# Two bilinear corner sums per sample instead of three, for a part of a deformable convolution's samples

## The chip, the cores and the metric

The kernel runs on one core of a Trainium2 chip (trn2). The metric is the device time of one execution in microseconds. The engines are written PE (TensorE), DVE (VectorE), ACT (ScalarE), POOL (GpSimd) and SP (SyncE); PEld is PE's weight load.

## The reference, cut to what matters

Four layers run one after the other on x of shape (2, 256, 64, 64) in float32, numbered 0 to 3: attention, a position term, a bottleneck with a deformable convolution, and the layer of this case, two deformable convolutions in a row:

```python
def bilinear_gather(x, py, px):
    y0, x0 = jnp.floor(py), jnp.floor(px)
    wy1, wx1 = py - y0, px - x0
    wy0, wx0 = 1.0 - wy1, 1.0 - wx1
    ...
    return (gather(y0, x0) * (wy0 * wx0)[:, None] + gather(y0, x0 + 1.0) * (wy0 * wx1)[:, None]
        + gather(y0 + 1.0, x0) * (wy1 * wx0)[:, None] + gather(y0 + 1.0, x0 + 1.0) * (wy1 * wx1)[:, None])

def deform_conv(x, dw, pw, pwb, w, b):
    f = lax.conv_general_dilated(x, dw, (1, 1), 'SAME', feature_group_count=C, dimension_numbers=dn)
    off = lax.conv_general_dilated(f, pw, (1, 1), 'SAME', dimension_numbers=dn)
    ...
    sampled = bilinear_gather(x, py, px)
    return jnp.einsum('bckhw,ock->bohw', sampled, w.reshape(O, C, KK)) + b[None, :, None, None]

h = deform_conv(jax.nn.relu(group_norm(x, gn1_g, gn1_b)), dw1, pw1, pwb1, w1, b1)
h = deform_conv(jax.nn.relu(group_norm(h, gn2_g, gn2_b)), dw2, pw2, pwb2, w2, b2)
return h + x
```

Each of 9 taps of each pixel is read at a fractional place: four neighbours, each with the product of a weight in y and a weight in x. The weights differ from pixel to pixel and are the same for all 256 channels.

## The kernel before, in words

The third layer is the method `deform`. It keeps the normalised image in memory as rows that hold, for a place, the 256 channels of two lines of the image, so that one indexed read of 4 KB per pixel brings all four corners: `four`, 128 pixels by 4 x 256 channels, in the order (left, upper), (left, lower), (right, upper), (right, lower). Such a tile is the unit of the work and is called a sample here: one tap for 128 pixels. `parts(s)` takes the number s of a sample apart: n is the convolution and image (four of them, `layers`: first convolution of image 0, of image 1, then the second of each), i one of 8 blocks of 512 pixels, k the tap and j the quarter of a block. There are 36 samples in a block, 288 in a convolution of an image, 1152 in all.

The order of work on PE, ACT, DVE and POOL is written out by hand: it is the order in which the program issues instructions, and each engine runs its own in that order. The loop at L1570 has one step for each s:

- `gather(s + 8)`: an indexed read on POOL's queue (line 846) into one of ten buffers `four`. The first two blocks of image 0 were sampled during layer 0 and come by plain transfers from `samp_d` on SP's queue instead.
- `first(s + 1)`: ACT multiplies corner 0 by its weight into a new tile `smp` (L1459); there are five such tiles.
- `others(s)`: DVE multiplies and adds corners 1, 2 and 3 one after the other (L1465).
- every fourth step `evacuate`: ACT copies four transposed samples from PSUM (L1486).
- `product`: PE multiplies with the convolution's weights (L1496, two instructions in the records for each call), then `turn(s - 2)`: PE transposes a sample (L1477, two instructions). A `turn` frees its `smp`.
- what is due: at the end of a block an activation (L1521) or a residual add on DVE (L1532).
- side work in small portions: the offsets of later blocks (`offsets`: PE at L803, L823 and L837, ACT at L814 and L832), from which `corners` computes indices and weights on DVE (L738 to L776); the next image (`image`: ACT L1370, PE L1380, DVE L1386); and at the start of the layer what remains of layer 2's deformable convolution for image 1 (`seconds`: POOL L846, DVE L1065 to L1076).

`corners` first has the weights by axis, `w` with one entry per side (0 is left or upper, 1 is right or lower) and axis (0 is y, 1 is x), and then the four products `w4`, of which `first` and `others` use one per corner. The tile `w` lies in a work pool and is overwritten by the next block but one; `w4` and the indices lie in a pool of four, `cp`.

Of the kernel before, what the change touches and what calls it, by code (L numbers as in the profile page):

```python
# [11 lines left out]
F32 = mybir.dt.float32  # L12
# [3 lines left out]
ALU = mybir.AluOpType  # L16
# [4 lines left out]
P = 128  # L21
B, C, H, W = 2, 256, 64, 64
# [3 lines left out]
K2 = 9  # L26
# [3 lines left out]
EARLY = 2  # L30
# [34 lines left out]
class Net:  # L65
# [662 lines left out]
                n += 2  # L728


    def corners(self, i, pt, mask, base, idx, w4, pool):

        nc = self.nc
        p = pool.tile([P, 4, K2, 2], F32, name="pos")
        off = pt[:, :, 0 : 2 * K2].rearrange("p j (k t) -> p j k t", t=2)
        nc.vector.tensor_tensor(p, off, base[:, 4 * i : 4 * i + 4], ALU.add)  # L738
        if mask:
            mk = pool.tile([P, 4, K2], F32, name="mask")  # L740
            nc.vector.tensor_scalar_max(mk, pt[:, :, 2 * K2 : 3 * K2], -87.0)
        yield False
        if mask:

            nc.scalar.activation(mk, mk, AF.Exp, scale=-1.0)

        nc.vector.tensor_scalar(p, p, float(H), -1.0, ALU.min, ALU.max)
        whole = pool.tile([P, 4, K2, 2], I32, name="whole")
        nc.vector.tensor_copy(whole, p)
        yield True  # L750
        f = pool.tile([P, 4, K2, 2], F32, name="floor")
        nc.vector.tensor_copy(f, whole)
        g = pool.tile([P, 4, K2, 2], F32, name="above")
        nc.vector.tensor_tensor(g, f, p, ALU.is_gt)
        yield False
        nc.vector.tensor_tensor(f, f, g, ALU.subtract)
        nc.vector.tensor_scalar_min(f, f, float(H - 1))
        w = pool.tile([P, 2, 4, K2, 2], F32, name="wt")
        nc.vector.tensor_tensor(w[:, 1], p, f, ALU.subtract)
        yield False  # L760
        nc.vector.tensor_scalar(w[:, 0], w[:, 1], -1.0, 1.0, ALU.mult, ALU.add)
        at = pool.tile([P, 4, K2], F32, name="at")
        nc.vector.scalar_tensor_tensor(
            at, f[:, :, :, 0], float(GW), f[:, :, :, 1], ALU.mult, ALU.add
        )
        nc.vector.tensor_scalar_add(idx, at, float(GW + 1))
        yield True
        if mask:
            nc.vector.tensor_scalar_add(mk, mk, 1.0)
            nc.vector.reciprocal(mk, mk)  # L770
            yield False
            for s in range(2):
                nc.vector.tensor_mul(w[:, s, :, :, 1], w[:, s, :, :, 1], mk)
            yield False
        for s in range(4):
            nc.vector.tensor_mul(w4[:, :, :, s], w[:, s % 2, :, :, 0], w[:, s // 2, :, :, 1])  # L776
        yield True
# [8 lines left out]
            ALU.mult,  # L786
        )

    def offsets(self, i, srcs, wt, bias, base, idx, w4, pool, wide, ps, odp=None, y0=0, later=lambda f: f()):

        nc, half, size = self.nc, DWK // 2, DWK
        m = size * 2 * K2
        pd = ps([P, 512])
        order = [half] + [t for t in range(size) if t != half]
        n = 0
        for s, src in enumerate(srcs):
            for t in order:  # L800
                y = 8 * i + t - half
                r0, r1 = max(0, -y), min(8, H - y)
                nc.tensor.matmul(  # L803
                    pd[:m, r0 * W : r1 * W],
                    lhsT=wt(s, t),
                    rhs=src[:, (y + r0 - y0) * W : (y + r1 - y0) * W],
                    start=(n == 0),
                    stop=(n == len(srcs) * size - 1),
                )
                n += 1  # L810
                yield "bank"

        later(
            lambda: nc.scalar.copy(  # L814
                wide[:m, :, half : half + W], pd[:m].rearrange("p (r w) -> p r w", w=W)
            )
        )
        yield
        pz = ps([P, 512])
        sums = pz.rearrange("p (r w) -> p r w", w=W)  # L820
        for t in range(size):
            g = t % 4
            nc.tensor.matmul(  # L823
                sums[32 * g : 32 * g + 32],
                lhsT=self.shift[:m, t, :],
                rhs=wide[:m, :, t : t + W],
                start=(t < 4),
                stop=(t + 4 >= size),
            )
        yield "bank"  # L830
        od = odp() if odp else pool.tile([P, 512], F32, name="od")
        later(lambda: nc.scalar.activation(od, pz, AF.Identity, bias=bias))  # L832
        yield

        pt = ps([P, 4, 32])
        for j in range(4):
            nc.tensor.matmul(  # L837
                pt[:, j, :], lhsT=od[:, j * P : (j + 1) * P], rhs=self.sel, start=True, stop=True
            )
        yield "bank"  # L840
        for _ in self.corners(i, pt, False, base, idx, w4, pool):
            yield

    def gather(self, dst, img, idx):
# [9 lines left out]
    class Bottleneck:  # L854
# [41 lines left out]
            self.od = wp.tile([P, 512], F32, name="bod")  # L896
            nc.gpsimd.memset(self.od, 0.0)

        def pools(self, ctx, gathers=5):
            self.ahead = gathers - 1  # L900
            tc = self.net.tc
            return self.kept | {
                n: ctx.enter_context(tc.tile_pool(name=f"bt_{n}", bufs=bufs))
                for n, bufs in (("g", gathers), ("s", 8), ("t", 6), ("x", 2))
            }

        def block(self, pool, src, i):
# [391 lines left out]
    def deform(self, bott):  # L1299
# [4 lines left out]
        tc, nc, a = self.tc, self.nc, self.a  # L1304
        with ExitStack() as ctx:
            gp = ctx.enter_context(tc.tile_pool(name="df_g", bufs=10))
            wp = ctx.enter_context(tc.tile_pool(name="df_w", bufs=1))
            work = ctx.enter_context(tc.tile_pool(name="df_work", bufs=2))
# [87 lines left out]
                        yield  # L1396

            IMAGE = 4 + 6 * NB + 1
            corners = {(0, 0, i): (None, w4) for i, w4 in self.early.items()}

            def offsets(b, l):
                if b == 0:
                    yield from offset_weights(l)
                wf = self.wf
                for i in range(EARLY if (b, l) == (0, 0) else 0, NB):
                    idx = cp.tile([P, 4, K2], I32, name="didx")
                    w4 = cp.tile([P, 4, K2, 4], F32, name="dw4")
                    corners[b, l, i] = idx, w4
                    yield from self.offsets(
                        i,  # L1410
                        [x[b][:, cb, :] for cb in range(2)],
                        lambda s, row: wf[:, s, DWK * row : DWK * row + DWK, :].rearrange(
                            "p t o -> p (t o)"
                        ),
                        self.vec[:, V_PWB + l : V_PWB + l + 1],
                        base, idx, w4, work, ods[i % 2], pd,
                    )

            ods = [wp.tile([P, 8, W + DWK - 1], F32, name=f"wide{n}") for n in range(2)]
# [10 lines left out]
            def parts(s):  # L1430
                n, r = divmod(s, LAYER)
                i, r = divmod(r, BLOCK)
                return n, i, r // 4, r % 4

            def gather(s):
                if s < ALL:
                    n, i, k, j = parts(s)
                    b, l = layers[n]
                    fours[s] = gp.tile([P, 4, C], F32, name="four")
                    four = fours[s].rearrange("p s c -> p (s c)")  # L1440
                    if n == 0 and i < EARLY:

                        queue = nc.gpsimd if s < AHEAD else nc.sync
                        m = 4 * k + j
                        queue.dma_start(four, self.samp_d[i][m * P : m * P + P, :])
                        return
                    idx = corners[b, l, i][0]
                    self.gather(four, self.img3[b], idx[:, j, k : k + 1])

            def weight(s, c):  # L1450
                n, i, k, j = parts(s)
                w4 = corners[(*layers[n], i)][1]
                return w4[:, j, k, c : c + 1]

            def first(s):

                if s < ALL:
                    smps[s] = sp.tile([P, C], F32, name="smp")
                    nc.scalar.mul(smps[s], fours[s][:, 0], weight(s, 0))  # L1459

            def others(s):
                if s < ALL:
                    four = fours.pop(s)
                    for c in range(1, 4):
                        nc.vector.scalar_tensor_tensor(  # L1465
                            smps[s], four[:, c], weight(s, c), smps[s], ALU.mult, ALU.add
                        )
# [83 lines left out]

            OFFS = 24
            inner = ExitStack()
            second = bott.conv(1, bott.pools(inner, 8), ps)
            for s in range(AHEAD):
                gather(s)
                conv_weight(0, s)
# [12 lines left out]
            for s in range(ALL + 12):  # L1570
                n = s // LAYER
                if s == LAYER:
                    stats[1] = self.norm_stats()
                gather(s + AHEAD)
                first(s + 1)
                others(s)
                if (s - 6) % 4 == 0:
# [126 lines left out]
```

## Time and profile before

| | us |
|---|---|
| median of 3 runs | 5151.03 (5145.72 to 5154.88) |
| profiled execution, first to last instruction (its span) | 5149.0 |
| DVE busy in it | 4196.7 (82%) |
| PE busy | 4816.8 (94%) |
| ACT busy | 2883.6 (56%) |
| POOL busy | 2254.7 (44%) |
| L1465, the three corner additions: 3240 + 216 instructions of 128x256 | 1503.8 + 104.4 |
| L1459, the first corner: 1080 + 72 of 128x256 | 535.9 + 34.3 |
| third layer's first sample, from the trace (L1459) | 2995.4 |

The busy time of an engine is the time in which at least one of its instructions runs; instructions of one engine can overlap at their ends. For PE the ends are modelled, so its busy share is not its share of peak. The profiled execution has no time of its own beside its span; the median of the runs stands 2 us above it. A windowed view gives busy time in a stretch, with the count of instructions in brackets.

### The profile page before, as it was taken

The page shows a single profiled execution, that of the slowest core. Times are in us where ns is not written, and L with a number is a line of the kernel's source. Part 1 is how long each engine was busy: PE and PEld are TensorE (multiplying, and loading weights), DVE is VectorE, ACT ScalarE, POOL GpSimd, SP SyncE. Part 2 cuts the span into 40 slices and gives each one's busy share as a digit, 9 for nine tenths or more (in the row PEclk, how much of TensorE's full clock was granted, in tenths as well). Part 3 has the DMA queues.
Part 4 walks back from the last instruction along what each step waited for, and adds up shares of the span by engine and source line. Part 5 has one row for each costly group of instructions (what it writes and reads, how often), then busy time and mean ns, then how long its engine had stood idle before and what let it go on. Part 6 is the DMA issues. An engine that isn't in the chain of part 4 may idle for free. (4 is left out here: it accounts for less than half of the span.)

```text
span 5149.0 us, 100000 instructions
## 1 busy us (share of the span) xinstructions
PE 4816.8 (94%) x38200; PEld 2651.9 (52%) x38200; DVE 4196.7 (82%) x7929; ACT 2883.6 (56%) x5221; POOL 2254.7 (44%) x2256
## 2 busy tenths in 40 slices
PE   8999999999999999999999957679999999999998
PEld 5555565555565555565555523234444444444443
DVE  6878867878668888687766768878999999999998
ACT  5666656666666666666656622235444554454444
POOL 0111111111107777464023257775666566666665
PEclk9999999999999999999999967789999999999999
DMA  5231121111113333322557677679999999999998
GB/s 172 61 99 51 42 68 49 35 46 30 55 52 94 93 100 102 94 85 79 150 193 272 233 242 239 207 251 376 340 329 339 360 359 350 356 388 346 347 348 318
DMA packets 367022, 997.66 MB, mean 194 GB/s; under 512 B 61372, under 2 KB 98810, under 8 KB 366542
## 3 DMA queue, kind: packets, MB, share of 16 engines
q0 software_dynamic: 196560, 690.41, 37.7%
q1 hardware_dynamic: 169438, 300.73, 17.9%
q8 instruction: 300, 4.92, 0.4%
q14 instruction: 180, 1.47, 0.1%
q10 hardware_dynamic: 544, 0.13, 0.0%
HBM read 855.36 MB, written 127.35 MB: 191 GB/s over the span
## 5 line engine op out<-in xcount | busy, mean ns | idle before, releaser
L1465 DVE SCALAR_TENSOR_TENSOR smp<-four,dw,smp 128x256 f32<-128x256 f32 x3240 | 1503.8, 483 | 122.3 <-ACT smp L1459 44.4
L598 ACT ACTIVATE e<-sc,low 128x1024 f32<-128x1024 f32 x1024 | 1147.1, 1120 | 745.1 <-DVE low L592 741.4
L592 DVE TENSOR_REDUCE low<-sc 128x1 f32<-128x1024 f32 x1024 | 1204.8, 1218 | 228.1 <-PE sc L580 224.0
L846 POOL DMA_INDIRECT four<-img,didx x1080 | 1085.4, 1005 | 646.3 <-DVE smp L1465 349.2
L1496 PE MATMUL out<-st,wc 128*128 128x512 f32 x2304 | 1229.6, 616 | 65.0 <-ACT st L1486 33.6
L580 PE MATMUL sc<-k,qs 64*128 64x512 f32 x2048 | 997.1, 605 | 1.8 <-ACT e L598 1.4
L639 PE MATMUL av<-et,v 128*64 128x256 f32 x8192 | 996.5, 385 | 0.0
L580 PE MATMUL sc<-k,q 64*128 64x512 f32 x2048 | 977.3, 604 | 0.0
L519 POOL TENSOR_TENSOR o<-o,f 128x1024 f32<-128x1024 f32 x63 | 149.3, 2370 | 1771.5 <-DMA f<-share_d 890.1
L610 PEld LDWEIGHTS tt<-ident,e 64*128 64x128 f32 x16384 | 651.7, 139 | 519.3 <-issue 275.4
L1459 ACT ACTIVATE smp<-four,dw 128x256 f32<-128x256 f32 x1080 | 535.9, 507 | 594.3 <-PE pt L1477 460.4
L610 PE MATMUL tt<-ident,e 64*128 64x64 f32 x16384 | 726.1, 226 | 40.5 <-ACT et L629 19.9
L629 ACT COPY et<-tt 128x512 f32<-128x512 f32 x1152 | 659.5, 586 | 170.5 <-PE tt L610 169.2
L627 DVE COPY et<-tt 128x512 f32<-128x512 f32 x896 | 612.0, 683 | 161.3 <-PE tt L610 160.9
L639 PEld LDWEIGHTS av<-et,v 128*64 128x64 f32 x8192 | 552.1, 137 | 302.9 <-issue 48.4
L1477 PEld LDWEIGHTS pt<-ident,smp 128*128 128x128 f32 x2304 | 320.5, 144 | 740.8 <-issue 423.4
L846 POOL DMA_INDIRECT bfour<-img,bidx x576 | 581.0, 1009 | 184.2 <-issue 90.3
L1496 PEld LDWEIGHTS out<-st,wc 128*128 128x128 f32 x2304 | 392.0, 196 | 323.3 <-issue 216.5
L1477 PE MATMUL pt<-ident,smp 128*128 128x128 f32 x2304 | 454.6, 280 | 72.7 <-DVE smp L1465 67.1
L580 PEld LDWEIGHTS sc<-k,qs 64*128 64x128 f32 x2048 | 345.4, 188 | 215.7 <-issue 120.0
L1486 ACT COPY st<-pt 128x1024 f32<-128x1024 f32 x288 | 291.2, 1011 | 289.5 <-PE pt L1477 287.8
L803 PE MATMUL pd<-x,wf 128*126 128x512 f32 x840 | 433.4, 598 | 0.0
(183 smaller groups left out, 3600.4 us busy)
## 6 DMA issues: line engine op xcount, KB each, us to landing
f<-share_d SPq DMA_DIRECT2D x128, 256.0 KB
four<-samp_d SPq DMA_DIRECT2D x64, 512.0 KB
xb<-xn SPq DMA_DIRECT2D x55, 512.0 KB
img<-imgt SPq DMA_DIRECT2D x96, 256.0 KB
four<-img,didx POOLq DMA_INDIRECT x1080, 6.1
xa<-res SPq DMA_DIRECT2D x32, 512.0 KB
samp_d<-xb SPq DMA_DIRECT2D x32, 512.0 KB
xb<-in_x SPq DMA_DIRECT2D x20, 512.0 KB
```

The costliest lines, as they stand in the source:

```text
L580: nc.tensor.matmul(s[:, j, :], lhsT=q[u, i // 2][int(h != j)][halves[j], at : at + P], rhs=k[u][c][halves[j], h, :], start=True, stop=True,)
L592: nc.vector.tensor_reduce(low, s, AX.X, ALU.max, negate=True)
L598: nc.scalar.activation(e.rearrange("p j n -> p (j n)"), s, AF.Exp, bias=blk.low[:, g, c : c + 1], accum_out=blk.sum[:, g, c : c + 1],)
L610: nc.tensor.transpose(pt[:, m, :], e[half, m // 4, m % 4 * P : m % 4 * P + P], self.ident[half, half],)
L627: nc.vector.tensor_copy(dst, pt)
L629: nc.scalar.copy(dst, pt)
L639: nc.tensor.matmul(now["av"][halves[h], :], lhsT=v[u][c][:, m, halves[h]], rhs=ets[j][:, m, h, :], start=(m == 0), stop=(m == 7),)
L846: self.nc.gpsimd.indirect_dma_start(out=dst, out_offset=None, in_=img, in_offset=bass.IndirectOffsetOnAxis(ap=idx, axis=0),)
L1459: nc.scalar.mul(smps[s], fours[s][:, 0], weight(s, 0))
L1465: nc.vector.scalar_tensor_tensor(smps[s], four[:, c], weight(s, c), smps[s], ALU.mult, ALU.add)
L1477: nc.tensor.transpose(pts[u][:, c, j * P : (j + 1) * P], smp[:, c * P : c * P + P], self.ident,)
L1496: nc.tensor.matmul(outs[ob], lhsT=wc[k][:, c, ob * P : ob * P + P], rhs=sts[u][:, c, :], start=(k == 0 and c == 0), stop=(k == K2 - 1 and ...
```

## The change

For a part of the samples the four corners are combined by axis. `left` has ACT multiply the two left corners in place by the weight of the left side in x (one instruction over 512 elements); `right` has DVE multiply the two right corners by the weight of the right side and add (one instruction over 512); then `first` has ACT multiply the upper row by its weight in y, and `others` has DVE multiply the lower row and add (256 each). This is done for all samples of blocks 2 to 7 in the first convolution of image 0, and for every second sample (odd j) of the three other passes. The rest stays as it was. In the loop, `left(s + 2)` and `right(s + 1)` stand ahead of `first(s + 1)` and `others(s)`.

For this the weights by axis must live as long as the indices: `w` becomes a tile `dwt` in the pool `cp` (four buffers, one per block) that `offsets` hands down to `corners`. In `corners` the tile `at` is no longer its own: the floor test's tile `g`, by then used up, holds the address sum. The pool of sums of layer 2's remaining work has seven buffers instead of eight.

```diff
-    def corners(self, i, pt, mask, base, idx, w4, pool):
+    def corners(self, i, pt, mask, base, idx, w4, pool, w=None):
...
-        w = pool.tile([P, 2, 4, K2, 2], F32, name="wt")
+        if w is None:
+            w = pool.tile([P, 2, 4, K2, 2], F32, name="wt")
...
-        at = pool.tile([P, 4, K2], F32, name="at")
+        at = g.rearrange("p j k t -> p (j k t)")[:, : 4 * K2]
+        at = at.rearrange("p (j k) -> p j k", k=K2)
...
+                    w = cp.tile([P, 2, 4, K2, 2], F32, name="dwt")
+                    corners[b, l, i] = idx, w4, w
...
+            def paired(s):
+                n, i, _, j = parts(s)
+                return s < ALL and (i >= EARLY if n == 0 else j % 2 == 1)
+
+            def share(s, side, axis):
+                n, i, k, j = parts(s)
+                w = corners[(*layers[n], i)][2]
+                return w[:, side, j, k, axis : axis + 1]
+
+            def left(s):
+
+                if paired(s):
+                    uv = fours[s][:, 0:2].rearrange("p s c -> p (s c)")
+                    nc.scalar.mul(uv, uv, share(s, 0, 1))
+
+            def right(s):
+                if paired(s):
+                    four = fours[s].rearrange("p s c -> p (s c)")
+                    uv = four[:, : 2 * C]
+                    nc.vector.scalar_tensor_tensor(
+                        uv, four[:, 2 * C :], share(s, 1, 1), uv, ALU.mult, ALU.add
+                    )
+
             def first(s):
 
                 if s < ALL:
                     smps[s] = sp.tile([P, C], F32, name="smp")
-                    nc.scalar.mul(smps[s], fours[s][:, 0], weight(s, 0))
+                    scale = share(s, 0, 0) if paired(s) else weight(s, 0)
+                    nc.scalar.mul(smps[s], fours[s][:, 0], scale)
 
             def others(s):
-                if s < ALL:
+                if paired(s):
+                    nc.vector.scalar_tensor_tensor(
+                        smps[s], fours.pop(s)[:, 1], share(s, 1, 0), smps[s], ALU.mult, ALU.add
+                    )
+                elif s < ALL:
...
-            second = bott.conv(1, bott.pools(inner, 8), ps)
+            second = bott.conv(1, bott.pools(inner, 8, 7), ps)
...
                 gather(s + AHEAD)
+                left(s + 2)
+                right(s + 1)
                 first(s + 1)
                 others(s)
```

## The prediction

> **What bounds the kernel now.** I read the page first, then the busy time by stage, then the order of time on single engines, because the shares of the page do not say which of three nearly full engines is the limit.
>
> ```profile
> PE 4816.8 (94%) x38200; PEld 2651.9 (52%) x38200; DVE 4196.7 (82%) x7929; ACT 2883.6 (56%) x5221; POOL 2254.7 (44%) x2256
> PE   8999999999999999999999957679999999999998
> DVE  6878867878668888687766768878999999999998
> DVE smp L1465 10%; PE out L1496 9%; PE pd L803 5%; PE pt L1477 2%; DMA bfour<-img,bidx 2%; DMA four<-img,didx 1%; DVE bfour L1065 1%; DVE bfour L1075 1%; PE pd L823 0%; ACT st L1486 0%; POOL bfour L846 0%; PE av L639 0%; DVE res L1532 0%; ACT smp L1459 0%; DVE imgt L1386 0%
> ```
>
> The third layer is the last 17 slices; from the 29th on PE and DVE both show 9, and the chain that ended last alternates between them. Busy time by stage (PE, PEld, DVE, ACT, POOL, then clock, DMA share, GB/s), and the same for line 1465 alone:
>
> ```profile
> 3335.00:3523.00 188.00, 142.81 (x473) 68.58 (x472) 149.94 (x358) 64.94 (x113) 131.24 (x127) 0.87 0.79 272
> 3523.00:3757.00 234.00, 225.22 (x841) 111.23 (x842) 220.56 (x516) 122.61 (x210) 146.53 (x145) 1.00 0.98 364
> 3987.00:4110.00 123.00, 115.60 (x452) 59.76 (x452) 115.57 (x278) 66.91 (x115) 72.53 (x72) 1.00 0.97 355
> 4573.00:5032.00 459.00, 439.05 (x1572) 213.88 (x1573) 426.64 (x1003) 217.76 (x377) 286.03 (x289) 1.00 0.96 353
> ...
> 4573.00:5032.00 459.00, 399.45 (x865) 1.00 0.96 353
> ```
>
> Three instructions of L1465 make a sample, so the last stretch passes 865/3 = 288.3 samples in 459 us: 1.592 us a sample. The order of time on DVE, PE and ACT gives what an instruction really occupies, from its start to the next start:
>
> ```profile
> 4695.83 1.52 DVE L1465 SCALAR_TENSOR_TENSOR smp<-four,dw,smp 128x256 f32<-128x256 f32 x3
> 4697.27 0.75 DVE L1532 SCALAR_TENSOR_TENSOR res<-out,vec,res 128x512 f32<-128x512 f32 x1
> 4697.93 1.52 DVE L1465 SCALAR_TENSOR_TENSOR smp<-four,dw,smp 128x256 f32<-128x256 f32 x3
> ...
> 4866.38 1.02 PE L1496 MATMUL out<-st,wc 128*128 128x512 f32 x2
> 4867.24 0.38 PE L1477 MATMUL pt<-ident,smp 128*128 128x128 f32 x2
> 4867.46 1.02 PE L1496 MATMUL out<-st,wc 128*128 128x512 f32 x2
> ...
> 4011.29 0.82 ACT L1370 ACTIVATE x<-x,gn_sh,gn_sc 128x512 f32<-128x512 f32 x1
> 4012.01 0.89 ACT L1459 ACTIVATE smp<-four,dw 128x256 f32<-128x256 f32 x2
> ```
>
> A sample's three instructions hold DVE from 4695.83 to 4697.27, 1.44 us. The first two, which the next one must wait for since it reads their result, take (1.52 - 0.485)/2 = 0.52 each; the third, followed by something independent, 1.44 - 1.04 = 0.40, less than its 0.485 of busy time because the next instruction starts before it ends. In the last stretch that makes 288.3 x 1.44 = 415 us, and DVE's other work there is 426.6 - 399.5 = 27: 442 of 459. **DVE is the limit.** PE is close behind. A pair of product matmuls holds it for 0.86 us (4866.38 to 4867.24), a pair of transposes for 0.22. By the groups of this stretch: 576 products at 0.43 are 248 us, 576 transposes at 0.11 are 63, 229 offset matmuls (L803) at 0.43 and some shorter 96, the small ones (L823, L837) 24: 431 of 459, 1.495 a sample.
>
> **What the change does to DVE.** Call the new instructions, for sample s: L (ScalarE scales the left two corners, 128x512), R (VectorE adds the right two, 128x512), F (ScalarE scales one row, 128x256), O (VectorE adds the other, 128x256). Samples with a pair: 6 blocks x 36 = 216 in the first image's first layer, and every second one of the other 864, so 432. The elements on DVE are the same (512 + 256 = 3 x 256); one instruction start goes, and so do both waits on the own result, since R(s+1), O(s) and what follows do not read one another. R is like L1532, in shape and operation: 4697.27 to 4697.93, 0.66. O as the last of a sample now: 0.40. A pair costs 1.06 against 1.44 and saves 0.38.
>
> Here a rule is to be weighed. The Trainium skill ("VectorE: DVE Perf Modes", "The DRAIN you can't avoid") has the next operation wait until the pipe is empty, and the formula for fp32 tensor_tensor in its section "The TRN2 errata", (N+151)/0.96 ns, gives 424 for 256 and 691 for 512. Chained or not would then be one, and a pair would save 3 x 424 - 424 - 691 = 157 ns. The rows show the overlap (0.40 against 0.52), so I take 0.38 and keep 0.16 as the lower end. The other end is bounded by the 0.485 + 0.75 of busy time, 1.24: 0.20 saved, within these. In the last stretch 0.38 x 144 pairs = 55 us: DVE falls from 442 to 387, or 1.34 a sample. PE's 1.495 then is the bound, and with 0.16 DVE and PE tie.
>
> **What it does to ACT.** Each pair adds L. There is no row for a scaling of 128x512 in SBUF; the nearest is L1370 (with a bias too), 0.80 busy and 0.72 until its follower. The same section of that page prices it at (224+512)/1.2 = 613 ns; it gives 400 for F, which the trace has at 507 (L1459). I take the row. It matters where every sample is a pair, 3523 to 3757: 234 us for 433/3 = 144 samples, 1.62 each. ACT there needs L 0.72 to 0.80, F 0.41 to 0.51, the evacuation E (L1486) 1.01/4 = 0.25 and about 0.12 for the image and offsets: 1.50 to 1.68. By the page's figures, 0.61 + 0.40 + 0.37, it would be 1.38 and hidden behind PE. By the row ACT is level with PE. I take 1.55, a gain of 0.07 x 144 = 10 us.
>
> Elsewhere ACT has 217.8 of 459 busy; 144 L at 0.80 make it 333, so its sum is covered. Its order is less so. ACT issues L(s+2), F(s+1), then every fourth time E. F(s+1) now waits for R(s+1), and E and the next L queue behind it; DVE's R waits for that L, and the samples of DVE queue behind R. Between the end of R(s+1) and the start of R(s+3) DVE has O(s) 1.44, O(s+1) 0.40 and some 0.2 of other work, 2.04; ACT has F, E, L, 0.51 + 0.91 + 0.72 = 2.14, or 1.23 without E. So DVE stands perhaps 0.1 to 0.4 us in every four samples, up to 0.10 a sample, 1.44 with the rest: still under PE's 1.495. If that cover goes, it costs the same 0.10.
>
> **Edits I cost at nothing.** The weights moved to their own four buffers follow the same life as the indices beside them. Reusing g for the sum of addresses adds at most an ordering of DVE with itself, among 128x72 operations of 0.2 us per block. The gathers keep their number, order and buffers; L asks for its gather one iteration before F did, while ACT waited only 2.9 us on gathers from 3750 to 5070. POOL passes a gather in 1.25 us where nothing holds it (3099.29 to 3100.54), below 1.495; DMA must go from 353 to about 370 GB/s, and 388 stands on the page. Seven instead of eight sums in the second layer matter only if transposes run over six steps late; PE waits for DVE there. From 3335 to 3523 gathers of two layers share POOL and ACT waits 80.9 us on them, so I give DVE's saving no value there, with -10 to +10 as bounds.
>
> **The sum**, in the profiled execution (span 5149.0; the median of the runs is 2 us more, which I add). PE at its slots plus 2% for its waits on E is 1.52 a sample. Three plain stretches (3757 to 3987, 4110 to 4449, 4573 to 5032; 1028 us, 1949/3 = 650 samples, 1.582): 650 x 0.06 = -40. Two stretches where the next image is made (247 us, 144 samples, 1.71; PE, DVE and ACT all have its copies on top, PE about 1.58): to 1.64, -10. The all-pair stretch: -10. The end (from 5032: no offset matmuls, DVE bound, a gather each 1.25 to 1.35): 0.1 x 72 = -7. Together -67: 5082, and **5083 us** with the 2.
>
> **Rivals.**
> - **Slower: ACT becomes a link in DVE's path.** Place: between R(s+1) and R(s+3), where E stands. It decides when DVE stands over 2 x 0.38 = 0.76 us in four samples. If nothing overlaps, F, E and L are 0.51 + 1.01 + 0.81 = 2.33 and two handovers (estimate 0.05 each) 2.43, so 0.39 over DVE's 2.04. E also waits for PE's transposes, now 84.6 us over 72 times in the last stretch, 1.17 each; if half of that falls into this gap, DVE stands 0.98, 0.245 a sample against 0.19 saved: +0.055 x 866 = +48, and the all-pair stretch at 1.70 adds +12: 5211. For it: ACT now idles on PE 137.9 us there. Against: if PE is late, DVE has time. Chance 0.15.
> - **PE is the bound already.** It is busy 439 of 459, and only what it waits for can be won. If new waits on E take that back: 5147. Against: its slots leave 28. Chance 0.10.
> - **The change saves less than it says**, 0.16 a pair: DVE 442 - 23 = 419, level with PE. Half of the gain, 5115. Chance 0.08.
> - **PE runs flat out**: 650 x 0.087 = -57, image stretches at 1.58 -19, all-pair stretch at 1.51 -16, end -12, mixed stretch -10: 5037. For it: part of PE's idle time is a wait for DVE's L1532 (18.3 us in the last stretch), which a faster DVE ends. Chance 0.15.
>
> **How the numbers follow.** The likeliest case has 0.52 and its own range is 5055 to 5115. The five cases give faster 0.52 + 0.08 + 0.15 = 0.75, same 0.10, slower 0.15; "same" is within 0.2% (10 us), about what a measurement of this kernel can tell. The range leaves out half of the slower case and a tenth below the flat-out case: 5022 to 5160.
>
> **What would show it.** Right: R near 750 ns, O near 485 and L near 800; DVE in the plain stretches from 96% down to about 88% by slots, PE at 98%; ACT's waits on DVE's R longer than the present 6.7 us, DVE's on L under 30 us in the last stretch. Wrong: a DVE wait on L over 0.19 us a sample, or PE waiting longer than before for the evacuation.

## The result: 0.5% slower

The changed kernel takes 5173.14 us (median of 4 runs, 5171.6 to 5187.72) against 5148.38: ratio 1.0053, 95% interval 1.0039 to 1.0067 (taken over the single runs, so not quite the ratio of the medians). Beside other kernels on a second occasion it was 1.0055 (1.0041 to 1.0069). The forecast was 5083, with 5022 to 5160 as its range. On some occasions, called the slower chip below, the kernel before takes 5312 to 5343 us, on the others, called the ordinary chip, about 5150, and every ratio is to the kernel before on the same occasion.

The page of the profile after, with the lines that answer to those of before:

```profile
PE 4812.2 (93%) x38200; PEld 2672.0 (52%) x38200; DVE 4012.2 (78%) x7281; ACT 3252.7 (63%) x5869; POOL 2322.8 (45%) x2256
...
DVE  6878767878668888687766778777778888888888
...
PE out L1527 12%; PE pd L805 6%; DVE smp L1496 3%; PE pt L1508 3%; DMA bfour<-img,bidx 2%; ACT st L1517 2%; DVE four L1477 1%; DMA four<-img,didx 1%; DVE bfour L1067 1%; ACT four L1471 1%; PE pd L825 1%; DVE smp L1490 1%; DVE bfour L1077 1%; POOL bfour L848 0%; ACT smp L1486 0%
...
L1477 DVE SCALAR_TENSOR_TENSOR four<-four,dwt 128x512 f32<-128x512 f32 x648 | 485.0, 748 | 285.5 <-ACT four L1471 284.1
...
L1486 ACT ACTIVATE smp<-four,dwt 128x256 f32<-128x256 f32 x648 | 327.5, 505 | 388.6 <-DVE four L1477 353.0
L1471 ACT ACTIVATE four<-four,dwt 128x512 f32<-128x512 f32 x648 | 463.6, 715 | 55.2 <-DMA four<-img,didx 54.9
```

DVE is busy 184 us less and its 9s are gone, ACT is busy 369 us more, and PE has the same 38200 instructions. The chain that ended last has less DVE (9% of the span, 14% before) and more PE and ACT. In the new names L1471 is L, L1477 is R, L1486 is F, L1490 is O, L1496 the three additions of a sample without a pair, L1508 the transposes, L1517 the evacuation E, L1527 the product and L1563 the residual add. The groups show the handing over: in the whole layer R waited 284 us for L, F 353 us for R.

What that does to PE is in the waits of PE from sample 288 to 1080, first before, then after (who waits, for whom, us in total, times, longest); the last two rows are the waits of F and R in the same stretch:

```profile
PE pt L1477 <- DVE smp L1465: 21.3, 38, 1.1
PE out L1496 <- DVE res L1532: 18.7, 15, 1.6
PE pm L1380 <- DVE imgt L1386: 7.4, 4, 2.2
PE out L1496 <- ACT st L1486: 1.6, 2, 1.2
PE pt L1477 <- DVE floor L756: 0.6, 2, 0.4
```

```profile
PE out L1527 <- ACT st L1517: 55.9, 38, 2.8
PE out L1527 <- ACT four L1471: 10.1, 7, 1.4
PE out L1527 <- DVE res L1563: 7.3, 7, 1.0
...
ACT smp L1486 <- DVE four L1477: 288.7, 351, 3.1
...
DVE four L1477 <- ACT four L1471: 178.8, 155, 3.2
```

PE's waits for DVE fell from 48 us to 7; those for ACT rose from 2 to 66, of which 56 are put down to E and 10 to L, which stands beside E in ACT's order. One of them, in the order of time of three engines, at the edge of a block:

```profile
4785.43 0.75 DVE L1477 SCALAR_TENSOR_TENSOR four<-four,dwt 128x512 f32<-128x512 f32 x1
...
4786.27 0.51 ACT L1486 ACTIVATE smp<-four,dwt 128x256 f32<-128x256 f32 x1 [2.28 <-DVE four L1477]
4786.69 0.99 ACT L1517 COPY st<-pt 128x1024 f32<-128x1024 f32 x1
...
4785.50 0.38 PE L1508 MATMUL pt<-ident,smp 128*128 128x128 f32 x2
...
4787.73 1.13 PE L1527 MATMUL out<-st,wc 128*128 128x512 f32 x2 [0.77 <-ACT st L1517]
```

R starts late because DVE has just done a residual add and steps of `corners`. F waits 2.28 us for it. E is queued behind F and starts at 4786.69, although the last transposes that it copies were done at 4785.88 (4785.50 + 0.38), and PE's product waits for E. In the kernel before F read no result of DVE; ACT waited 22 us for DVE there in the same stretch, against 289 now.

### The profile page after: what moved, and what is told of

Its sections match the earlier page's. It is cut to its first block, busy times and chain, and to the rows that moved or that the text cites. A ratio compares the mean times of both kernels' runs of the same rounds, so it can differ in the third digit from the quotient of the medians.

```text
span 5172.1 us, 100136 instructions
## 1 busy us (share of the span) xinstructions
PE 4812.2 (93%) x38200; PEld 2672.0 (52%) x38200; DVE 4012.2 (78%) x7281; ACT 3252.7 (63%) x5869; POOL 2322.8 (45%) x2256
## 5 line engine op out<-in xcount | busy, mean ns | idle before, releaser
L848 POOL DMA_INDIRECT four<-img,didx x1080 | 1149.3, 1064 | 604.9 <-ACT smp L1486 192.0
L1527 PE MATMUL out<-st,wc 128*128 128x512 f32 x2304 | 1240.6, 621 | 148.5 <-ACT st L1517 124.0
L1477 DVE SCALAR_TENSOR_TENSOR four<-four,dwt 128x512 f32<-128x512 f32 x648 | 485.0, 748 | 285.5 <-ACT four L1471 284.1
L1508 PEld LDWEIGHTS pt<-ident,smp 128*128 128x128 f32 x2304 | 332.1, 145 | 668.3 <-issue 482.7
L1496 DVE SCALAR_TENSOR_TENSOR smp<-four,dw,smp 128x256 f32<-128x256 f32 x1296 | 627.2, 484 | 30.8
L1527 PEld LDWEIGHTS out<-st,wc 128*128 128x128 f32 x2304 | 393.2, 197 | 416.9 <-issue 202.7
L1486 ACT ACTIVATE smp<-four,dwt 128x256 f32<-128x256 f32 x648 | 327.5, 505 | 388.6 <-DVE four L1477 353.0
L1471 ACT ACTIVATE four<-four,dwt 128x512 f32<-128x512 f32 x648 | 463.6, 715 | 55.2 <-DMA four<-img,didx 54.9
L1508 PE MATMUL pt<-ident,smp 128*128 128x128 f32 x2304 | 451.9, 279 | 29.6 <-DVE smp L1496 29.6
```

Source lines behind the costliest of these rows:

```text
L848: self.nc.gpsimd.indirect_dma_start(out=dst, out_offset=None, in_=img, in_offset=bass.IndirectOffsetOnAxis(ap=idx, axis=0),)
L1477: nc.vector.scalar_tensor_tensor(uv, four[:, 2 * C :], share(s, 1, 1), uv, ALU.mult, ALU.add)
L1496: nc.vector.scalar_tensor_tensor(smps[s], four[:, c], weight(s, c), smps[s], ALU.mult, ALU.add)
L1508: nc.tensor.transpose(pts[u][:, c, j * P : (j + 1) * P], smp[:, c * P : c * P + P], self.ident,)
L1527: nc.tensor.matmul(outs[ob], lhsT=wc[k][:, c, ob * P : ob * P + P], rhs=sts[u][:, c, :], start=(k == 0 and c == 0), stop=(k == K2 - 1 and ...
```

## What the time is made of

In the stretch from PE's transposes of sample 287 to those of 1079, on the ordinary chip and in one profiled execution each, PE's listed waits account for the difference:

| kernel | us | PE waits for DVE | for ACT | the rest |
|---|---|---|---|---|
| before | 1274.6 | 48.0 | 1.6 | 1225.0 |
| after | 1295.7 | 7.3 | 66.0 | 1222.4 |
| after, second time | 1297.7 | 7.3 | 67.8 | 1222.6 |
| e2_fourth (pair one step earlier) | 1262.8 | 7.7 | 34.2 | 1220.9 |
| e12_again (that, no pairs in the first pass) | 1261.4 | 7.7 | 34.9 | 1218.8 |

The rest, time less waits, is nearly the same in these five executions: 1219 to 1225 us for 792 samples, 1.54 us a sample, whatever DVE and ACT do. It holds PE's own work and what a list of waits cannot show: a product lasts 0.59 us in the records and the next starts after 0.43, so a delay under 0.16 us leaves no gap. In e6 and e7 below, which have equal work on PE, the rest is 1157 and 1107, so it is not PE's work alone. By the listed waits, about 50 us could be won here, and the change exchanged 41 us of waits for DVE for 64 us of waits for ACT.

## The experiments

The kind of chip is named with each run. On the slower one PE and ACT also show waits with no releaser, named "issue" in the rows.

**Is PE or DVE the bound? Take work from PE.** Half of the offset matmuls are left out, of the kernel before (e6) and of the changed one (e7), so their offsets come from half of the channels; the changed kernel itself (after_again) ran beside them (ordinary chip).

```diff
-                nc.tensor.matmul(
-                    pd[:m, r0 * W : r1 * W],
...
-                    stop=(n == len(srcs) * size - 1),
-                )
+                if odp or s == 0:
+                    nc.tensor.matmul(
+                        pd[:m, r0 * W : r1 * W],
...
+                        stop=(n == (len(srcs) if odp else 1) * size - 1),
+                    )
```

> The changed kernel again, as the measure for the three others on the same chip: 1.003 to 1.008 of the kernel before under every theory.

> The kernel before with half of the offset matmuls of the third layer left out (L803: seven of fourteen per block, about 6.0 us of PE in each of 30 blocks, 180 us; the offsets are those of half the channels). Theory A (PE sets the pace, DVE close behind): falls by 30 to 70 us, until DVE's 1.54 a sample binds. If DVE bound each sample, as the prediction had it: less than 12 us.

> The changed kernel with the same half of the offset matmuls left out. Theory A (PE's own work plus its waits on E make the 1.615 a sample): falls by 80 to 150 us, more than the kernel before does, since DVE has more room. Theory D (the loop F, E, L on ACT and R, O on DVE has a period of its own of about 1.6): falls by less than 30 us.

Measured: after_again 1.0055. The kernel before with half the offsets 0.9944 (0.9931 to 0.9958), 5122.43 us: 29 less, just short of the 30 expected. The changed kernel with half the offsets 0.9893 (0.9877 to 0.9908), 5095.66 us, 81 less than after_again. Both gain, so PE's work is part of the pace of both. The kernel before gains only 29 us from about 180 us of matmuls left out (the estimate above), because it soon meets DVE (1.55 us a sample in plain blocks, PE waiting 35.2 us for DVE's samples and 34.3 for the residual add). The changed one goes to 1.516, and there PE waits more on ACT than before:

```profile
PE out L1528 <- ACT st L1518: 98.8, 95, 2.8
PE out L1528 <- ACT four L1472: 10.8, 8, 1.4
...
ACT smp L1487 <- DVE four L1478: 299.9, 358, 3.1
```

So the change does give DVE room: with less work on PE it is 27 us faster than the kernel before, with PE's full work 25 us slower.

**What is relief of DVE worth without a handover?** The kernel before without corner 3 (e3, slower chip):

```diff
-                    for c in range(1, 4):
+                    for c in range(1, 3):
```

> The kernel before with corner 3 left out of every sample (two additions instead of three, ACT unchanged): what relief of DVE is worth when nothing is handed between the engines. Theory A: PE's waits on DVE in the third layer (63 us in the kernel before) are all there is to win: 5085 to 5120. If DVE were the bound of each sample, as the prediction had it, the 0.52 us of 1152 samples take it down to PE's floor by that reckoning, 5035 to 5085. If DVE relief is worth nothing: 5140 to 5150.

Measured: 0.9909 (0.9892 to 0.9925), about 48 us less, in Theory A's range when taken over to 5149 us (5102). An estimate of the DVE work removed is 1152 x 0.52 = 600 us (DVE's busy time fell by 520), more than twice the 648 x 0.38 = 246 us of the change. PE's waits on DVE's additions are gone from its list of samples 288 to 1080:

```profile
PE out L1496 <- ACT st L1486: 20.5, 12, 3.6
PE out L1496 <- issue: 10.8, 10, 4.6
PE pm L1380 <- ACT x L1370: 2.8, 1, 2.8
```

Additions that take 0.52 us of DVE each were worth 0.04 us a sample: DVE was nearly full, but most of its time was not the kernel's.

**Is it the order in which F meets R?** L and R one step earlier. The runs e2_pair_ahead, e2_again and e2_third (slower chip) and e2_fourth (ordinary chip) are the same kernel; after_third and before_look are the changed kernel and the one before, both beside e2_third:

```diff
-                left(s + 2)
-                right(s + 1)
+                left(s + 3)
+                right(s + 2)
```

> The changed kernel with left and right issued one step earlier (left(s+3), right(s+2)), so that F finds R done. Theory A: F's waits on R fall from 327 us to under 100, PE's waits on E under 30, time 5105 to 5140. Theory B: ACT has the same work, PE's waits on E stay above 50, 5160 to 5180. Theory C: the gather is needed a step sooner, so 5175 to 5195.

> The changed kernel with left and right one step earlier, again, beside other kernels on one chip. Theory A: 0.995 to 0.999 of the kernel before, as the first time (0.9971), so the handover is worth about 0.8% of the changed kernel. If that was the chip: 1.002 or more.

> left and right one step earlier. Theory A: 0.5 to 1.0% under after_third, 0.995 to 0.999 of the kernel before. If the order is worth nothing: as after_third.

> The changed kernel beside the same with the pair one step earlier. Theory A: 1.004 to 1.007 of the kernel before, on any chip. If the gain of the earlier pair was the chip's and not the order's: equal to e2_third within 0.2%.

> The kernel before, for its trace on this chip: PE's waits in samples 288 to 1080 for DVE about 48 us and for ACT under 5 us if what bounds it is the same on every chip.

> left and right one step earlier, on a chip that is hoped to be one where the kernel before takes about 5150 us. There the changed kernel has 1.0053 and 1.0055. Theory A (F's wait for R delays E and with it PE): 0.994 to 1.001. If the order is worth nothing there either, as on the other chip (0.9966 against 0.9973): 1.004 to 1.007.

On the slower chip it was first 0.9971 and 0.9977, but that said nothing of the order: on another occasion of that kind the changed kernel itself was 0.9973 (0.9963 to 0.9983), faster than the one before, and the earlier pair beside it 0.9966 (0.9956 to 0.9977), no different. Theory A's number for after_third was wrong there. The order did take F's wait for R from 211 us to 52 on that chip, but PE's wait for E only from 52 to 47, so PE gained little by it. On the ordinary chip it was 0.9986 (0.9979 to 0.9993), 5141.39 us, against 1.0053 and 1.0055 for the change as it was: about 34 us for the same kernel in another order, though on another occasion. ACT's busy time is the same (3254 us, 3253 in the change), so its load is not what cost the time. F's wait for R fell from 289 us to 60, and PE's wait for E from 56 to 30 (samples 288 to 1080 of e2_fourth):

```profile
PE out L1527 <- ACT st L1517: 30.3, 33, 2.0
PE out L1527 <- DVE res L1563: 7.3, 7, 1.0
...
ACT four L1471 <- DMA four<-img,didx: 89.0, 96, 2.5
ACT smp L1486 <- DVE four L1477: 59.5, 69, 2.5
```

The third of these rows is the price: L needs its gather a step sooner and waits 89 us for it, in front of F and E; in the change as it was, L waited 0.4 us for gathers from 3532 us on.

before_look, on the slower chip, has PE's waits of the ordinary chip (22.7 us for the samples, 19.1 for the residual add, 5.8 for E) and others on top whose releaser is not shown: 16.2 us of PE's, 60 of ACT's. Its stretch takes 1307 us instead of 1275, that of the changed kernel 1300 instead of 1296, that of the earlier pair (e2_third) 1295 instead of 1263. So the kernel before and the earlier pair lose 32 us each there and the changed kernel 4. Most of the change's other ratio on that chip lies in this stretch, as far as single executions tell. Room on DVE does not explain it, since the earlier pair has the same, and the cause stays open.

**Is it ACT's load?** L left out (e4), R and F as they are (the left corners are not scaled):

```diff
-                    nc.scalar.mul(uv, uv, share(s, 0, 1))
+                    pass
```

> The changed kernel with L left out (the left corners are not scaled), R and F as they are. Theory A: F still waits for R in DVE's order and E behind F, but R waits no more for L: 5120 to 5155. Theory B: ACT's load is that of before, 5090 to 5120. Theory C: unchanged, 5165 to 5180.

Measured on the slower chip: 0.9969 (0.9956 to 0.9981), against 0.9973 for the changed kernel on the slower chip on another occasion. Without L's work on ACT (464 us in the change) the time is the same, which speaks against Theory B. Theory A's picture was wrong too: F's wait for R fell to 34 us (211 in after_third), which suggests that most of that wait came from L through R, and PE's wait for E only to 43 (52). On the ordinary chip L was not left out; there e2_fourth, with all of L's work, speaks against the load.

**Can the evacuation be put in front?** (e1)

```diff
                 gather(s + AHEAD)
+                if (s - 6) % 4 == 0:
+                    evacuate((s - 6) // 4)
                 left(s + 2)
...
-                if (s - 6) % 4 == 0:
-                    evacuate((s - 6) // 4)
```

> The changed kernel with evacuate (ACT's copy E) issued at the start of a step, ahead of left and first, instead of behind first. Theory A (PE is the bound; E stands on ACT behind F, F waits for R on DVE, and PE's product waits for E): PE's waits on E from 3532 us on fall from 79.3 us to under 25, time 5105 to 5135, below the kernel before. Theory B (ACT simply has 464 us more to do with L, and E is late because ACT is loaded): the waits stay above 50, time 5160 to 5180. Theory C (the loss lies in gathers and the mixed stretch, not on ACT): 5165 to 5180.

Measured on the slower chip: 1.0011 (1.0001 to 1.0022), above the 0.9973 that the changed kernel later had on a chip of that kind. PE's waits for E did fall in samples 288 to 1080, to 28.4 us (from 3560 us on they are 70.2, where under 25 was expected), but E now waits for PE at the head of ACT's queue (211 us) and F stands behind it: DVE's O waits 116 us for F, and the residual add comes late again (PE waits 20.1 us for it). The wait moved one engine on. Theory A's forecast for this run was wrong.

**Due work first, and L last.** In the kernel before, what is due in a step is issued at its start (e9). Then the changed kernel with that, with R a step earlier and with L behind F and E, three things at once (e10, the edit shown), and the same without pairs in the first pass (e11).

```diff
                 gather(s + AHEAD)
+                for f in due.pop(s, ()):
+                    f()
-                left(s + 2)
-                right(s + 1)
+                right(s + 2)
                 first(s + 1)
                 others(s)
                 if (s - 6) % 4 == 0:
                     evacuate((s - 6) // 4)
+                left(s + 3)
                 product(*divmod(s - 7, 4), s)
                 turn(s - 2)
-                for f in due.pop(s, ()):
-                    f()
```

> The kernel before with what is due in a step (residual add on DVE, activation, statistics) issued at the start of the step instead of its end. Theory A (PE paces; of its 66 us of waits in the third layer 23 are for the residual add, which frees the bank of the product): 5149 to 5120 or 5138. If DVE's sum bound every sample: within 6 us of the kernel before.

> The changed kernel with right one step earlier, left issued last in the step (behind F and E) for the sample three ahead, and what is due at the start of the step. Theory A (what ACT does for DVE must not stand ahead of what PE waits for): PE's waits on E and on the residual add under 25 us together in samples 288 to 1080, 5075 to 5115, faster than both kernels. Theory B (ACT's load): 5150 or more.

> The same without pairs in the first pass. The changed kernel lost 5 us by the all-pair pass: 3 to 8 us below the one before it if that loss stands there too; above it if, with the order mended, all pairs pay in the first pass.

All on the slower chip, and all misses of Theory A. e9: 1.0004 (0.9994 to 1.0014); PE's waits for the residual add fell from 19.1 us (before_look, another occasion) to 9.4, those for the samples rose from 22.7 to 28.1, and the time did not move. This is what the rival (DVE's sum binds every sample, within 6 us) had forecast; e3 speaks against that rival, and e9 alone does not settle it. e10: 1.0018 (1.0008 to 1.0027), slower than e2_again beside it (0.9977). Its waits in samples 288 to 1080 suggest why:

```profile
PE out L1527 <- ACT st L1517: 64.2, 44, 2.9
...
ACT smp L1486 <- DVE four L1477: 220.8, 239, 3.4
...
DVE four L1477 <- ACT four L1471: 164.7, 125, 3.8
```

Issued behind F and E, L comes late for R (164.7 us of waits), the step won between R and F is lost between L and R, and PE waits 64 us for E, where 25 for E and the residual add together was expected. e11, without pairs in the first pass, 1.0036 (1.002 to 1.0051), slower still where it should have been faster; that is not explained.

**Which part of the pairs costs?** No pairs in the first pass, with the order as in the change (e5), and then with the earlier order (e12, e12_again):

```diff
-                return s < ALL and (i >= EARLY if n == 0 else j % 2 == 1)
+                return s < ALL and n > 0 and j % 2 == 1
```

> The changed kernel with no pairs in the first pass (only every second sample of the three later passes). The changed kernel had lost 6.7 us to the kernel before at sample 288 and 20 after it. Theory A (the same handover everywhere): the part up to sample 288 is that of the kernel before within 3 us, and the whole 0.1% faster than the changed kernel. Rival (the second layer's seven sums cost the early loss): no change before sample 288.

> left and right one step earlier, and no pairs in the first pass. If the all-pair pass still costs, 2 to 6 us under e2_third and faster than both kernels; if its pairs pay with the earlier order, above e2_third.

> The same without pairs in the first pass. 0.1 to 0.3% below e2_fourth, by what the all-pair pass cost in e5 (1.0055 to 1.0037). If the pairs of the first pass pay with the earlier order: above e2_fourth.

e5: 1.0037 (1.0023 to 1.0051), 7 us under after_again (the two intervals overlap), of which 5 by sample 288. In single executions, the part up to there takes 769.2 us from the layer's first transpose; the change takes 773.4 and 774.2, the kernel before 763.4. So about half of the early loss is the pairs'; the other 5.8 us stand without any pair, and their cause was not found (the seven sums and the moved tiles are candidates that were not tried alone).

e12 on the slower chip: 0.996 (0.9947 to 0.9972), no different from e2_third's 0.9966. On the ordinary one, e12_again: 0.9972 (0.9961 to 0.9983), 5133.83 us, against 5141.39 for e2_fourth beside it. Pairs in later passes only, with two steps between L and F instead of one, beat both kernels: 15 us under the one before.

## Why the prediction was wrong

The parts of the sum, forecast and measured (traces before and after, borders by PE's transposes):

| part | forecast, us | measured, us |
|---|---|---|
| plain stretches | -40 | +21 (1048.9 against 1028.0) |
| two stretches with the next image | -10 | 0 (246.8 against 246.5) |
| all-pair stretch, samples 144 to 288 | -10 | +1 (236.3 against 235.5) |
| mixed stretch, samples 72 to 144 | 0, bounds of 10 | +6 (196.2 against 190.6; 193.3 without its pairs, e5) |
| the end, last 72 samples | -7 | -5 (99.3 against 103.9; PE has no offset matmuls there) |

- **ACT's order is covered by PE's 1.495.** This step failed, and it turned the sign. The text saw that F waits for R, that E stands behind F and L behind E, but it priced the stand on DVE alone, 0.10 us a sample at most, and held that to be covered. It did not follow E to the engine that waits for it. DVE's stand for L was 179 us from sample 288 to 1080, 0.23 a sample; PE's waits for ACT rose by 64 us there, 0.08 a sample, more than the 41 us of waits for DVE that went. Both signs of being wrong that the prediction named came true.
- **DVE is the limit.** This step failed too. DVE's slots did fill 442 of 459 us, but with another engine at 431 that sum says little of what DVE's relief is worth. PE's waits said more: 48 us for DVE in samples 288 to 1080. e3 took about 600 us off DVE and gained about 48; e6 took about 180 us off PE and gained 29, until DVE held it.
- **PE's floor, 1.495 a sample and 1.52 with waits.** Mis-sized. In the three plain stretches of the kernel before PE's listed waits are 7.1, 10.1 and 18.6 us, so time less waits is (1028 - 35.8)/650 = 1.53 us a sample. The 1.52 left no room for any wait on E: the forecast gain of 0.06 a sample was as much as the end of every wait could give (35.8/650 = 0.055).
- **A pair saves 0.38 us of DVE.** Right: R is 748 ns and occupies 0.66 (4785.43 to 4786.09, where the next addition starts), O occupies 0.40. The 0.16 by the rule of the pipe that must be empty was not met: what is independent starts before its predecessor ends. The section that the prediction cites for the rule ("The DRAIN you can't avoid") itself adds that a next operation that is not held starts earlier, which is what these rows show. The saving was made and could not be spent.
- **L at 0.80, from L1370.** Too high: 715 ns. The 613 by the figures of the Trainium skill ("VectorE: DVE Perf Modes", "The TRN2 errata") was too low, as its 400 is for F, which takes 505. No part of the outcome is known to hang on it.
- **The slower rival** named the right place, the gap between R(s+1) and R(s+3) with E in it, but it counted DVE's standing as the loss, where PE's waits for E made it, and it had twice the loss (5211).

## What to carry over

When two engines are both nearly full, their sums do not tell what relief is worth: list what each waits for. Here PE waited 48 us for DVE, and about that much came of taking 600 us off DVE. Before a step is given to a second engine that also feeds the pacing one, write down its queue and ask what the new wait holds up behind it. On the ordinary chip two steps of distance between the parts of the chain, instead of one, turned +0.5% into -0.1%, and leaving out the pass in which every sample has the chain made it -0.3%.

## Not expected of the hardware

The sign of the change differs between occasions: 1.0053 where the kernel before takes 5150 us, 0.9973 where it takes 5343. Whether it is the chip or its condition is open: the record gives the number 13 to a chip of each kind. Up to the first gathers the two profiles of the kernel before run in step (0.6 us apart at 1440 us); at 1588 us, among these gathers, the slower one is 10 us behind, 55 us by the start of the third layer and 187 at its end, while the gathers' packets take the same 159 ns at the median. The clock granted to PE is not the cause in samples 288 to 1080: it was 1.00 in both, and the slower execution took 32 us more.

Independent DVE additions of 128x256 start 0.40 us apart and chained ones 0.52, so an instruction's busy time of 0.485 is neither.
